# Scaling the normed rows of layer 1 on ACT instead of DVE

## The chip, the cores and the metric

The kernel runs on one core of one Trainium2 chip. The metric is device time in microseconds (us), the median of several runs. A core has five engines that run side by side, each with its own queue in program order: PE (TensorE, matrix products and transposes), DVE (VectorE), ACT (ScalarE), POOL (GpSimd) and SP, which here issues the DMAs.

## The reference

The input x has 8 images of 256 channels and 32 x 32 positions, all in float32. Layer 0 is a convolution and attention block on images. Layer 1 sees each image as 1024 tokens of 256 values and adds two branches to them, each behind a layer norm without weights:

```python
def _ln_t(v, eps=1e-5):
    m = jnp.mean(v, axis=-1, keepdims=True)
    s = jnp.var(v, axis=-1, keepdims=True)
    return (v - m) / jnp.sqrt(s + eps)

t = _to_tokens(x)
t = t + _L1_attn_ref(_ln_t(t), L1_attn_WQ, L1_attn_WK, L1_attn_WV)
t = t + _L1_ffn_ref(_ln_t(t), ...)
x = _from_tokens(t, x)
```

`_L1_attn_ref` is causal attention with one head over the 1024 tokens of an image. `_L1_ffn_ref` is a mixture of 8 experts of three products each, gated per token by a softmax over the mean of the normed tokens of all images. The change touches only the norm, `(v - m) / sqrt(s + eps)`.

## The kernel before

The kernel is written with a tile framework that places semaphores; every engine keeps the order in which the program issues its instructions. `pe`, `dve`, `act` and `pool` are thin wrappers that fix that order, and since all of them pass through one helper, almost all instructions have the line L73 in the profile. They are told apart by the tiles that they write and read.

Images are kept with the channels on the 128 partitions, in two halves (`KC` = 2), and the tokens along the free dimension. `layer_norm(src, dst, zt, room, bank)` norms the 1024 tokens of an image (8 rows of 128 tokens; two late calls take 4 rows) in these steps. PE transposes two rows at a time into a PSUM tile `tpt`, ACT copies it to `zt` (`zt_e` in the profile, one buffer for all calls; `scratch` in the last call), where a token is a partition. DVE takes mean and variance of each row (`st`, then `mv`). POOL makes the factor `r` = (variance + eps)^-0.5 for all rows at once, with one power and a step of refinement, six instructions on 8 columns, using the tile `y` on the way. Then `scaled(i0)` makes two rows `(row - mean) * factor` in place. PE transposes them back into `tpz`, and ACT copies `tpz` to `dst` (`z_e`, `z` or `z_last`).

`layer_norm` is a generator. Its steps are issued between those of a main stream by `together`, which weighs both by the microseconds that they yield. In layer 1's attention the main stream is `causal(b)`: eight score rows i of 128 queries for image b. For each, PE makes the scores `s`, DVE takes their negated maximum `nm`, ACT the exponential `pr`, DVE masks it (`lower`), sums it and inverts the sum (`rs`), POOL scales `pr` by `rs`, PE transposes it (`tp`), ACT copies that to `pT`, and every second row PE makes the product `po`, which DVE adds to the image (`te` or `t`). `tp` and half of the `tpt` and `tpz` tiles share one pair of PSUM buffers; `po`, `pk`, `pv` and the other half of `tpt` and `tpz` share another.

Beside image b's scores run, in this order, the first norm of image b + 1 (`first_norm`), the second norm of image b - 1 (`second_norm`), and the keys and values of image b + 1 (PE `pk`, `pv`, ACT copies `kk`, `v`); between them chores that split the experts' weights (`parts_w`). After a second norm POOL adds the normed image to `feat` in two halves, and ACT and DVE split it in two parts for the experts (`parts` on ACT, a subtraction to `parts` on DVE, then `z`):

```python
yield from layer_norm(t[b], z2, early["zt"], room, bank)
nc.sync.dma_start(u_d[b], t[b])
...
for h, feat in enumerate(feats):
    half = z2[:, :, h * HALF : (h + 1) * HALF]
    if b == 0:
        pool.tensor_copy(feat, half)
    else:
        pool.tensor_add(feat, feat, half)
```

The first norm of image 0 runs earlier, beside the end of layer 0 (PE `ph`, `py`, `rbn`, DVE `xn` there). The last image takes its score rows in reverse, beside the second norm of image 6 and then a norm of its own upper half (`last_norm`); its lower half is normed beside the first experts (`last_half`). After 2128 us the experts alone remain.

Of the kernel before, what the change touches and what calls it, by code (L numbers as in the profile page):

```python
# [12 lines left out]
AF = mybir.ActivationFunctionType  # L13
ALU = mybir.AluOpType
# [91 lines left out]
def conv_attn_hybrid_kernel(  # L106
# [368 lines left out]
    pe, dve = InOrder(tc, nc.tensor, TensorCost()), InOrder(tc, nc.vector, vector_cost)  # L475
    act, pool = InOrder(tc, nc.scalar), InOrder(tc, nc.gpsimd)
# [4 lines left out]
    def layer_norm(src, dst, zt, room, bank):  # L481

        n = src.shape[2] // P
        mv = room([P, NT, 2], "mv", 2)
        for i0 in range(0, n, 2):
            tp = bank([P, 2, C], "tpt")
            for i in range(2):
                for k in range(KC):
                    c0 = (i0 + i) * P
                    pe.transpose(tp[:, i, k * P : (k + 1) * P], src[:, k, c0 : c0 + P], ident)  # L490
            act.copy(zt[:, i0 : i0 + 2, :], tp)
            yield 0.6
            for i in range(i0, i0 + 2):
                st = room([P, 6], "st", 4)
                dve.bn_stats(st, zt[:, i, :])
                dve.bn_aggr(mv[:, i, :], st)
            yield 0.6

        y = room([P, NT], "y1", 2)[:, :n]
        r = room([P, NT], "r1", 2)[:, :n]  # L500
        pool.tensor_scalar(y, mv[:, :n, 1], LN_EPS, None, ALU.add)
        pool.tensor_tensor(r, y, mhalf1[:, :n], ALU.pow)
        pool.tensor_mul(y, y, r)
        pool.tensor_mul(y, y, r)
        pool.tensor_scalar(y, y, -0.5, 1.5, ALU.mult, ALU.add)
        pool.tensor_mul(r, r, y)

        for _ in range(4):
            yield 1.0

        def scaled(i0):
            for i in range(i0, i0 + 2):
                dve.tensor_scalar(zt[:, i, :], zt[:, i, :], mv[:, i, 0:1], r[:, i : i + 1], ALU.subtract, ALU.mult)

        scaled(0)
        yield 1.0
        scaled(2)
        yield 1.0
        for i0 in range(0, n, 2):
            if i0 + 4 < n:  # L520
                scaled(i0 + 4)
            tp = bank([P, KC, 2, P], "tpz")
            for i in range(2):
                for k in range(KC):
                    pe.transpose(tp[:, k, i, :], zt[:, i0 + i, k * P : (k + 1) * P], ident)
            act.copy(dst[:, :, i0 * P : (i0 + 2) * P], tp.rearrange("p k i c -> p k (i c)"))
            yield 0.9
# [42 lines left out]
    def first_tokens(early, bank, bank_kv):  # L570
        return (
            layer_norm(t[0], early["z"], early["zt"], early["room"], bank),
            keys_values(early["z"], early["kk"], early["v"], early["at"], early["wv"], bank_kv),
        )
# [798 lines left out]
    def tokens(stack, early, early_stack):  # L1373
# [85 lines left out]
        with ExitStack() as l1:  # L1459
# [94 lines left out]
            def first_norm(b):  # L1554
                z[b] = ring(b, "z", [P, KC, N])
                yield from layer_norm(t[b], z[b], early["zt"], room, bank)
# [12 lines left out]
            def second_norm(b):  # L1569
                yield from until((b, N // QC - 1))  # L1570
                z2 = two.tile([P, KC, N], F32, tag="z2", name="z2", bufs=1)
                yield from layer_norm(t[b], z2, early["zt"], room, bank)
                nc.sync.dma_start(u_d[b], t[b])
                if b + 3 < B:
                    load_t(b + 3)
# [6 lines that stand above are left out]
                for h in range(2):  # L1582
                    yield from z_parts(b, h, z2[:, :, h * HALF : (h + 1) * HALF])
# [473 lines left out]
```

## Time and profile before

| | us |
|---|---|
| median of 3 runs | 3111.16 |
| lowest, highest | 3108.97, 3123.86 |
| the profiled execution, and its span | 3114.98, 3113.2 |
| PE, DVE busy in the span | 2935.5 (94%), 2394.0 (77%) |
| ACT, POOL busy in the span | 1562.5 (50%), 311.1 (10%) |
| layer 1's attention, PE busy from 1470 to 1545 us | 71.77 of 75.00 |

The span is from the first to the last instruction of one execution. A group in the profile is a line, an engine, an operation, its tiles as out<-in, shapes and a count, then the busy time and the mean of one in ns, and behind a second bar the engine's idle time before them and who ended it. The chain is the sequence of waits that ended last, followed back from the end; a row in it has a start, a duration and the engine with its tile. A timeline row has a start, a duration, the engine, the instruction and a count of equal ones in a row, with the idle time before it in brackets. TensorE's granted clock is a share of its full speed.

### The profile page before, as it was taken

To read this page: it belongs to the slowest core of one execution; us is meant where nothing else is said; L and a number is where in the kernel's file an instruction comes from. 1 tells how busy PE (TensorE), PEld (TensorE's weight loads), DVE (VectorE), ACT (ScalarE), POOL (GpSimd) and SP (SyncE) were. 2 spreads that over 40 slices of the span, in tenths; PEclk is the share of its full clock that TensorE was granted. 3 is DMA by queue.
4 is the path that set the end of the run, shared out by engine and by line. 5 is a ranking of instruction groups with operands and counts; after the bars stand their busy time and mean duration, and the time that the engine had idled before them with its cause. 6 is when DMAs were issued, how large, how long until landed. Compare 5 with 4: busy or idle time off the path is not lost.

```text
span 3113.2 us, 41565 instructions
## 1 busy us (share of the span) xinstructions
PE 2935.5 (94%) x16802; PEld 1944.3 (62%) x16802; DVE 2394.0 (77%) x3014; ACT 1562.5 (50%) x2312; POOL 311.1 (10%) x419
## 2 busy tenths in 40 slices
PE   6988999999899989889999999899999999999998
PEld 4544555555555555456666666677777777777776
DVE  2378787878787879776676765698988888888887
ACT  3554454545454545333333333465666666666664
POOL 1012111111111110001122222000000000000000
PEclk8999999999999999989999999999999999999999
DMA  6202121211212120003332311411221152112210
GB/s 193 54 2 69 41 66 44 58 52 53 57 47 63 40 57 21 30 29 113 134 133 108 122 65 60 183 68 68 95 75 68 68 188 89 68 68 88 81 68 29
DMA packets 63856, 234.87 MB, mean 75 GB/s; under 512 B 5590, under 2 KB 13862, under 8 KB 54822
## 3 DMA queue, kind: packets, MB, share of 16 engines
q1 hardware_dynamic: 63654, 232.12, 22.8%
q8 instruction: 134, 2.20, 0.3%
q14 instruction: 68, 0.56, 0.1%
HBM read 140.61 MB, written 91.49 MB: 75 GB/s over the span
## 4 chain that ended last, share of the span: by engine, by line
PE 81%; DVE 13%; ACT 3%; DMA 1%; issue 1%; POOL 1%; SPq 0%; ACTq 0%; DVEq 0%
PE pm L73 12%; PE pa L73 11%; PE q L73 11%; PE po L73 11%; PE s L73 8%; PE ph L73 6%; DVE o L73 4%; PE pq L73 3%; PE sums L73 3%; PE pz L73 2%; DVE x L73 2%; PE pv L73 2%; PE pk L73 2%; PE pp L73 2%; DVE conv L73 1%; DVE zt_e L73 1%
## 5 line engine op out<-in xcount | busy, mean ns | idle before, releaser
L73 PE MATMUL pa<-ze,w 128*128 128x512 f32 x1488 | 423.1, 393 | 0.0
L73 DVE SCALAR_TENSOR_TENSOR x<-hpad,vec,x 128x1024 f32<-128x1024 f32 x248 | 316.7, 1283 | 73.2 <-ACT x L73 65.8
L73 DVE SCALAR_TENSOR_TENSOR conv<-hpad,vec,conv 128x1024 f32<-128x1024 f32 x256 | 327.4, 1282 | 19.0 <-ACT conv L73 12.9
L73 PEld LDWEIGHTS pa<-ze,w 128*128 128x128 f32 x1488 | 278.2, 188 | 63.3 <-issue 3.0
L73 ACT ACTIVATE h<-pa,bn_o,s1a 128x512 f32<-128x512 f32 x256 | 198.6, 776 | 203.4 <-PE pa L73 203.4
L73 ACT ACTIVATE pT<-s 128x1024 f32<-128x1024 f32 x256 | 247.9, 1024 | 93.7 <-PE s L73 93.5
L73 PE MATMUL po<-pT,vT 128*32 128x256 f32 x4096 | 271.0, 382 | 0.0
L73 PE MATMUL q<-h2p,w 128*128 128x512 f32 x768 | 269.0, 459 | 0.0
L73 DVE SCALAR_TENSOR_TENSOR h<-pa,s1b,h 128x512 f32<-128x512 f32 x256 | 191.2, 747 | 93.6 <-PE pa L73 85.5
L73 PE MATMUL ph<-xn,piw 128*128 128x512 f32 x512 | 239.9, 610 | 8.3 <-ACT x L73 4.0
L73 PE MATMUL pm<-h,w 128*128 128x512 f32 x512 | 240.8, 592 | 0.0
L73 PE MATMUL q<-z_first,w 128*128 128x512 f32 x768 | 217.1, 391 | 2.8 <-DVE z_first L73 1.7
L73 PE MATMUL pm<-h1p,w 128*128 128x512 f32 x768 | 216.7, 390 | 0.5 <-DVE h1p L73 0.5
L73 PEld LDWEIGHTS q<-h2p,w 128*128 128x128 f32 x768 | 144.6, 188 | 83.1 <-issue 59.3
L73 DVE SCALAR_TENSOR_TENSOR o<-vpad,pe_w,o 128x1024 f32<-128x1024 f32 x128 | 163.6, 1282 | 39.4 <-ACT o L73 36.3
L73 PE MATMUL s<-qst,kst 128*128 128x256 f32 x1024 | 177.1, 317 | 7.2 <-ACT pT L73 4.5
L73 PEld LDWEIGHTS po<-pT,vT 128*32 128x32 f32 x4096 | 120.0, 109 | 84.0 <-issue 2.4
L73 PEld LDWEIGHTS s<-qst,kst 128*128 128x128 f32 x1024 | 140.8, 199 | 44.9 <-issue 30.4
L73 PEld LDWEIGHTS ph<-xn,piw 128*128 128x128 f32 x512 | 92.7, 193 | 121.7 <-issue 97.8
L73 PEld LDWEIGHTS q<-z_first,w 128*128 128x128 f32 x768 | 144.4, 188 | 34.3 <-DVE z_first L73 2.9
L73 PEld LDWEIGHTS pm<-h1p,w 128*128 128x128 f32 x768 | 144.7, 188 | 31.7 <-DVE h1p L73 0.9
L73 PE MATMUL sums<-pT,ones 128*32 128x256 f32 x2048 | 157.4, 379 | 0.0
(280 smaller groups left out, 5121.1 us busy)
## 6 DMA issues: line engine op xcount, KB each, us to landing
ze<-zd SPq DMA_DIRECT2D x29, 1536.0 KB, 6.4
qst<-part SPq DMA_DIRECT2D x32, 512.0 KB, 9.5
kst<-part SPq DMA_DIRECT2D x32, 512.0 KB, 16.0
te<-ud SPq DMA_DIRECT2D x32, 512.0 KB, 4.1
wd<-parts_w SPq DMA_DIRECT2D x20, 768.0 KB, 3.7
w<-wd SPq DMA_DIRECT2D x20, 768.0 KB, 5.5
zd<-parts SPq DMA_DIRECT2D x14, 1024.0 KB, 3.8
ud<-te SPq DMA_DIRECT2D x18, 512.0 KB, 3.3
```

Source lines behind the costliest of these rows:

```text
L73: return self._tc.keep_in_program_order(method(*args, **kwargs))
```

## The change

After the factor POOL makes a term, minus mean times factor, for all rows with two further instructions on 8 columns, in the tile `y` that it used before. The two rows of `scaled` are then made by ACT, as row times factor plus term with factor and term as column operands, and no longer by DVE. It applies to every call of `layer_norm`, 128 rows in all.

```diff
@@ -504,13 +504,15 @@
         pool.tensor_mul(y, y, r)
         pool.tensor_scalar(y, y, -0.5, 1.5, ALU.mult, ALU.add)
         pool.tensor_mul(r, r, y)
+        pool.tensor_mul(y, mv[:, :n, 0], r)
+        pool.tensor_scalar(y, y, -1.0, 0.0, ALU.mult, ALU.add)
 
         for _ in range(4):
             yield 1.0
 
         def scaled(i0):
             for i in range(i0, i0 + 2):
-                dve.tensor_scalar(zt[:, i, :], zt[:, i, :], mv[:, i, 0:1], r[:, i : i + 1], ALU.subtract, ALU.mult)
+                act.activation(zt[:, i, :], zt[:, i, :], AF.Identity, bias=y[:, i : i + 1], scale=r[:, i : i + 1])
 
         scaled(0)
         yield 1.0
```

## The prediction

> **What bounds the kernel now.** I read the page's totals and chain first, then the groups of the row scaling and of what could do it on ACT, then the chain and the timeline of one image's stretch in layer 1. The page:
>
> ```profile
> PE 2935.5 (94%) x16802; PEld 1944.3 (62%) x16802; DVE 2394.0 (77%) x3014; ACT 1562.5 (50%) x2312; POOL 311.1 (10%) x419
> PE 81%; DVE 13%; ACT 3%; DMA 1%; issue 1%; POOL 1%; SPq 0%; ACTq 0%; DVEq 0%
> L73 DVE TENSOR_SCALAR zt_e<-zt_e,mv,r 128x256 f32<-128x256 f32 x124 | 61.9, 558 | 10.8 <-POOL r L73 10.8
> L73 DVE TENSOR_SCALAR zt_e<-zt_e,mv,r x124: 394/402/2423, 1280.4 to 1964.8; 128x256 f32<-128x256 f32 x124
> ```
>
> PE bounds the whole; DVE is 13% of the chain. The scaled rows (124 in zt_e and 4 in scratch) take 402 ns in the median, but 558 in the mean and 2423 at worst: something holds some of them. Layer 1's attention runs from 1395 to 1967 us, an image about every 75 us. In each stretch two norms run beside the scores: the first norm of the next image and the second norm of the previous one. The chain of waits, and the timeline (start, duration, engine, instruction), where a second norm ends:
>
> ```profile
> 1562.76 1.77 DVE zt_e L73 x4
> 1564.52 1.15 DVE nm L73
> ...
> 1568.37 3.58 DVE zt_e L73 x3
> 1571.95 0.14 issue
> 1572.08 1.09 PE tpz L73 x4
> 1573.17 3.96 PE po L73 x16
> ```
> ```profile
> 1568.28 3.98 DVE L73 TENSOR_SCALAR zt_e<-zt_e,mv,r 128x256 f32<-128x256 f32 x4
> 1568.54 0.91 POOL L73 TENSOR_SCALAR pr<-pr,rs 128x768 f32<-128x768 f32 x1 [4.80 <-DVE rs L73]
> 1569.42 2.37 POOL L73 TENSOR_TENSOR feat<-feat,z 128x1024 f32<-128x1024 f32 x1
> 1572.08 1.09 PE L73 MATMUL tpz<-ident,zt_e 128*128 128x128 f32 x4 [1.99 <-DVE zt_e L73]
> 1573.87 2.36 POOL L73 TENSOR_TENSOR feat<-feat,z 128x1024 f32<-128x1024 f32 x1 [2.08 <-ACT z L73]
> 1575.68 1.63 DVE L73 TENSOR_TENSOR parts<-z,parts 128x1024 f32<-128x1024 f32 x1 [2.29 <-ACT parts L73]
> ```
>
> From 1553 to 1572 us DVE is the chain, with 1.8 + 3.6 us of scaled rows in it, and PE stands still for most of 1567 to 1572. The rows that last 1.0 and 2.4 us coincide with POOL's pr and feat. This recurs near 1643, 1718, 1793 and 1869 us (second norms of images 1 to 5); for image 0 the chain shows 2.27 us there, its feat being a short copy. The first norms are the other kind; between the scores the chain is PE alone:
>
> ```profile
> 1533.37 2.08 DVE L73 TENSOR_SCALAR zt_e<-zt_e,mv,r 128x256 f32<-128x256 f32 x6 [1.07 <-POOL r L73]
> 1534.69 0.60 PE L73 MATMUL tpz<-ident,zt_e 128*128 128x128 f32 x4
> 1537.72 1.05 PE L73 MATMUL tpz<-ident,zt_e 128*128 128x128 f32 x8
> ```
>
> Here DVE's rows are just in time and cost nothing.
>
> **The change part by part.** *Removed:* 128 rows from DVE, 0.33 us from one to the next when unheld. *Added on ACT:* 128 activations of 256 columns with two column operands. The trace has none; nearest is conv<-ph with both operands at 512 columns, 771 ns; less 256 columns at 0.83 ns (h<-h 625 at 512, x<-x 1050 at 1024) gives 558; from o<-vpad, 1236 at 1024, 599. I take 585. ACT's pairs overlap by about 0.1 (two copies of 0.59 in 1.07), so 0.49 from row to row: eight rows are 4.0 us of ACT. The total, some 70 us, lies beside other work in a half-idle engine; only its place in the queue matters. *Added on POOL:* two operations on 8 columns before the rows may start; the like ones last 0.20 and start 0.28 apart: 0.56 us later. No DMA is added or moved. No table load: Identity on yr and hi alternates with Exp in layer 0, and the kernel has 17 loads in all.
>
> The Trainium skill speaks against this ("ScalarE: Activation LUTs", Rules for kernel authors: multiply and add belong on VectorE). By it, each norm loses 8 x (0.49 - 0.33) + 0.56 = 1.8 us wherever its rows are on the path; 16 norms, 29 us slower, about 3140. The trace says otherwise for the second norms: there the eight DVE rows cost 5.4 us of chain. So I replay each kind on the trace's times.
>
> *Second norms, images 1 to 5.* POOL's factor is ready at 1562.42, its term at 1563.0. ACT, idle since 1561.55, does four rows by 1565.1 and then the pr that was at 1565.75, from 1565.0: 0.7 earlier. The two DVE-row groups vanish; pr, one pT copy, rows 4 and 5, a z copy and rows 6 and 7 follow on ACT until 1568.8, so PE turns the last rows at 1568.9 in place of 1572.1 and starts po 3.6 earlier. The granted clock, 0.75 from 1570 to 1573 and 0.68 to 1576 after PE's pause, need not fall either: po then lasts 3.1 and not 4.0. PE alone would gain 4.5. But look at what is late next. ACT's parts ends at 1572.2, and DVE's parts subtraction then meets the second feat of POOL, which now starts at 1571.8, straight after the first. The 1.63 above is 0.54 of waiting for feat and 1.09 of work; at 1941.0 the same subtraction took 2.88 beside feat. The Trainium skill ("SBUF — State Buffer", SBUF: two separate sides) has an exclusive lock between GpSimd and a DVE operation with two SBUF inputs, held for a whole instruction, ACT having its own ports: so rows on ACT are never held, but the subtraction is held to 1574.1. Without the lock the sum is 4.5 per image, with it this: subtraction done 1575.2, te, lower, the masked row and z done 1578.6, so nm of the last score row starts at 1578.6, before at 1581.14. Behind it on ACT are pr and the kk copy for which PE's third pk group waits (PEld waited 0.50 for it at 1584.87). Gain 2.5 each: 12.5.
>
> *Second norm of image 0:* the feat copies (1.09, 1.04) are over before the subtraction; gain 2.7.
>
> *First norms, images 2 to 7.* POOL's term comes at 1533.9, rows 0 and 1 end at 1535.05, PE wanted them at 1534.69: 0.4 lost. Rows 2 to 5 hold up z, pr and two pT copies; the first pT copy ends at 1538.35, not 1537.63, and frees the PSUM tile that PE wants at 1538.1: 0.25 more. Nothing later in the stretch gives it back, since PE is the chain until 1552. 6 x 0.65 = 3.9 lost. Bounds: 0, if the order of the tiles spares the second wait and POOL is quicker, and 4.5, all of ACT's 4.0 and POOL's 0.56. *Image 1's* (1410 us) is DVE's chain with rows lengthened by pr (0.68, 0.79 for 0.40): tpz at 1415.99 becomes free of waits, 0.9 gained.
>
> *Second norm of image 6* (the last stretch, scores in reverse) is already a POOL-to-rows-to-copies chain:
>
> ```profile
> 1935.03 2.67 DVE L73 TENSOR_SCALAR zt_e<-zt_e,mv,r 128x256 f32<-128x256 f32 x8 [2.16 <-POOL r L73]
> 1936.91 1.56 ACT L73 COPY z<-tpz 128x512 f32<-128x512 f32 x3 [3.26 <-PE tpz L73]
> 1939.40 3.44 PE s L73 x8
> ```
>
> Rows and copies now share ACT: rows 0 to 5 from 1935.6 to 1938.6, the third z copy to 1941.1 in place of 1938.5, so the scores start 2.6 later; with PE idle that long I add 0.9 for a half-clock stretch: 3.5 lost.
>
> *The rest:* image 0's first norm at 1281 us: 0.3 lost (POOL's delay; DVE's xn comes earlier). The two half norms: about 0.4 lost together, covered mostly by PE; without cover they cost 2 x (2.0 + 0.56) = 5.
>
> Sum: 12.5 + 2.7 + 0.9 - 3.9 - 3.5 - 0.7 = 8.0 us faster. The profiled execution took 3114.98 (span 3113.2); less 8.0 it is 3107. The median of the runs, 3111.16, lies 3.8 lower; from it: 3103.
>
> **The rivals.** *No lock in the way:* the subtraction gets in before the second feat, or ACT's rows are quicker, and PE's 4.5 comes through: 5 x 4.5 + 3.2 + 0.9 - 3.9 - 3.5 - 0.7 = 18.5, time 3093. For it: at image 6 the subtraction asked during the first feat (1941.0) and its end, 1943.9, less 1.09 of work, says that it was let in at 1942.8, between the two. Against: parts is four ACT operations (2.8 us) behind the z copy that starts feat (2.4 us), so it comes 0.4 us too late.
>
> *ACT's queue becomes the bound of the first norms* (the slower side): six rows stand in front of z, pr and the pT copies, and PE waits for these in order. At the full price of 4.5 each, 11.9 - 6 x 4.5 = 15 slower (11.9 is the sum without first norms' loss), time 3126; were the second norms' gain lost too (pr behind the rows there as well), 3141. It decides from 2.0 us a norm on, where 11.9 is used up. For it: the waits of PE there are zero now and ACT serves PE's tiles. Against: ACT had 3.2 us free before z there, and PE has 16 transposes and 8 score matmuls in between.
>
> *It doesn't reach the path at all:* DVE's order after 1572 is kept by other waits (te after po), so second norms gain what first norms lose; 3111.
>
> **How the numbers follow.** This kernel's measurement can tell about 0.5%, 15.6 us: faster is below 3095.6, slower above 3126.7. My forecast (3097 to 3109) has 0.45, the path unmoved (3108 to 3116) 0.15, no lock 0.24, ACT's queue 0.16. Of the forecast's chance 0.04 lies below 3095.6, of the queue's 0.12 above 3126.7, of the unmoved 0.01. The range reaches into both sides: 3089 to 3124.
>
> **What would show it.** In the changed profile: a row on ACT near 585 ns; no DVE TENSOR_SCALAR on zt_e; PE's wait before the last tpz of a second norm under 1 us where it was 1.99; parts on DVE 2.5 to 3.0 us instead of 1.63; the half-clock stretches of images 1 to 5 gone; PE waiting about 2 us in pk for ACT's kk copy; in first norms a PE wait of 0.4 for ACT zt_e; stretches near 73.2 us in place of 75.1. I am wrong if these stretches keep 75 us, or if first norms show PE waits over 2 us.

## The result and the profile after

The changed kernel takes 3104.35 us in the median of 21 runs (3098.13 to 3113.97), the kernel before 3114.41 in 21 runs beside it (3107.97 to 3127.12). The ratio is 0.9966, with a 95% interval of 0.9956 to 0.9975: 8 to 14 us faster, the middle near 10.6. The profiled executions are 12.1 us apart in span (3113.2 and 3101.1). The page after, and the new rows among the groups of tile zt_e (duration in ns: least, median, most):

```profile
PE 2927.2 (94%) x16802; PEld 1930.9 (62%) x16802; DVE 2339.8 (75%) x2886; ACT 1620.6 (52%) x2440; POOL 316.8 (10%) x453
PE 74%; DVE 14%; ACT 6%; POOL 2%; DMA 2%; issue 1%; SPq 0%; ACTq 0%; DVEq 0%; POOLq 0%
L73 ACT ACTIVATE zt_e<-zt_e,y,r x124: 583/588/614, 1280.0 to 1954.6; 128x256 f32<-128x256 f32 x124
```

A row on ACT is slower than the unheld row on DVE (588 against 402 ns), but none is long: the worst is 614, where DVE's worst was 2423. DVE has 54 us less to do and ACT 58 more, yet PE still bounds the kernel. The page cannot say where 10 us went; the timeline of the second norm of image 1 can (the place shown before at 1568 to 1577):

```profile
1561.22 2.08 ACT L73 ACTIVATE zt_e<-zt_e,y,r 128x256 f32<-128x256 f32 x4 [1.47 <-POOL y L73]
1566.57 0.93 PE L73 MATMUL tpz<-ident,zt_e 128*128 128x128 f32 x4 [0.53 <-ACT zt_e L73]
1567.55 4.68 POOL L73 TENSOR_TENSOR feat<-feat,z 128x1024 f32<-128x1024 f32 x2 [0.62 <-ACT z L73]
1570.32 3.00 DVE L73 TENSOR_TENSOR parts<-z,parts 128x1024 f32<-128x1024 f32 x1 [3.33 <-ACT parts L73]
1575.01 3.60 PE L73 MATMUL pk<-z,at 128*128 128x512 f32 x8
1576.73 1.22 DVE L73 TENSOR_REDUCE nm<-s 128x1 f32<-128x1024 f32 x1
1580.44 3.70 PE L73 MATMUL pk<-z,at 128*128 128x512 f32 x8 [1.83 <-ACT kk L73]
```

PE's wait for the last rows fell from 1.99 us to 0.53. But POOL's two additions to feat now run back to back, DVE's subtraction, which asks during the second of them, grew from 1.63 to 3.00 us, and PE, which used to run through pk, stands 1.83 us in it. The chain of waits in this stretch shows how the two are joined:

```profile
1570.32 3.00 DVE parts L73
...
1575.58 1.23 DVE z L73
1576.81 1.15 DVE nm L73
...
1578.04 1.11 ACT pr L73
1579.15 0.75 ACT pT L73 x2
1579.90 0.50 ACT kk L73
1580.40 0.04 issue
1580.44 3.70 PE pk L73 x8
```

The subtraction holds up nm of the last score row, nm the exponential, and the kk copy stands behind that in ACT's queue. So a good part of the gain became a new wait. The first norms, which had no wait on PE, now have a small one (timeline of the first norm of image 3, the place shown before at 1533 to 1538):

```profile
1531.47 3.06 ACT L73 ACTIVATE zt_e<-zt_e,y,r 128x256 f32<-128x256 f32 x6 [1.82 <-POOL y L73]
1532.24 0.81 PE L73 MATMUL tpz<-ident,zt_e 128*128 128x128 f32 x4
1535.89 1.09 PE L73 MATMUL tpz<-ident,zt_e 128*128 128x128 f32 x8 [0.24 <-ACT pT L73]
```

To add this up I take, from the profiled executions, the time from the first pk of one image to that of the next, with the start of layer 1's scores ahead and the first lg (the gate) behind. "Chosen", "later" and "both" are experiments told below.

| from, to | before | after | chosen | later | both |
|---|---|---|---|---|---|
| scores, image 1 | 28.60 | 27.57 | 27.54 | 27.57 | 27.32 |
| image 1, 2 | 84.82 | 82.36 | 81.71 | 82.37 | 81.69 |
| image 2, 3 | 74.83 | 70.96 | 70.34 | 71.00 | 70.30 |
| image 3, 4 | 74.96 | 72.79 | 72.13 | 71.11 | 70.35 |
| image 4, 5 | 75.03 | 72.74 | 72.11 | 71.00 | 70.32 |
| image 5, 6 | 75.06 | 72.79 | 72.16 | 71.04 | 70.36 |
| image 6, 7 | 75.38 | 74.58 | 73.07 | 72.84 | 71.28 |
| image 7, gate | 85.68 | 89.84 | 87.48 | 89.79 | 86.21 |
| sum | 574.36 | 563.63 | 556.53 | 556.72 | 547.83 |

Of the 12.1 us between the spans, 10.7 lie here. The stall in pk comes after an image's first pk, so it counts to the next line: image 2 to 3 shows the gain without it (3.9 with the first norm's loss), image 7 to the gate a stall that belongs to image 5's norm.

### The profile page after: what moved, and what is told of

Its sections match the earlier page's. It is cut to its first block, busy times and chain, and to the rows that moved or that the text cites. A ratio compares the mean times of both kernels' runs of the same rounds, so it can differ in the third digit from the quotient of the medians.

```text
span 3101.1 us, 41593 instructions
## 1 busy us (share of the span) xinstructions
PE 2927.2 (94%) x16802; PEld 1930.9 (62%) x16802; DVE 2339.8 (75%) x2886; ACT 1620.6 (52%) x2440; POOL 316.8 (10%) x453
## 4 chain that ended last, share of the span: by engine, by line
PE 74%; DVE 14%; ACT 6%; POOL 2%; DMA 2%; issue 1%; SPq 0%; ACTq 0%; DVEq 0%; POOLq 0%
PE pm L73 12%; PE pa L73 11%; PE q L73 11%; PE po L73 9%; PE s L73 6%; PE ph L73 6%; DVE o L73 4%; PE pq L73 3%; PE sums L73 3%; DVE conv L73 3%; DVE x L73 2%; PE pz L73 2%; ACT zt_e L73 2%; PE pv L73 2%; PE pp L73 1%
```

## The experiments

**Which norms gain.** In four kernels a call of `layer_norm` says whether ACT or DVE makes its rows; POOL makes the term only for ACT. What they share, shown with the choice of the first:

```diff
-    def layer_norm(src, dst, zt, room, bank):
+    def layer_norm(src, dst, zt, room, bank, on_act=False):
...
+        if on_act:
+            pool.tensor_mul(y, mv[:, :n, 0], r)
+            pool.tensor_scalar(y, y, -1.0, 0.0, ALU.mult, ALU.add)
...
+                if on_act:
+                    act.activation(zt[:, i, :], zt[:, i, :], AF.Identity, bias=y[:, i : i + 1], scale=r[:, i : i + 1])
+                else:
+                    dve.tensor_scalar(zt[:, i, :], zt[:, i, :], mv[:, i, 0:1], r[:, i : i + 1], ALU.subtract, ALU.mult)
...
-                yield from layer_norm(t[b], z[b], early["zt"], room, bank)
+                yield from layer_norm(t[b], z[b], early["zt"], room, bank, False)
...
-                yield from layer_norm(t[b], z2, early["zt"], room, bank)
+                yield from layer_norm(t[b], z2, early["zt"], room, bank, b < 6)
```

*Second norms of images 0 to 5.* 

> ACT scales the rows only in the second norms of images 0 to 5, DVE everywhere else. Theory (the terms of the prediction are separate and add up): 5 x 2.5 + 2.7 = 15.2 us faster than before, ratio near 0.9951, and faster than the full change by 5 to 7 us; stretch from one image's first pk to the next about 72.2 us. Rival A (the gain comes from DVE being relieved as a whole, wherever its rows lie): about half of the full change's gain, 5 us, ratio 0.9984. Rival B (the second norms gain nothing by themselves; the stretches are shorter for another reason, such as image 1's norm or the clock): within 2 us of before.

Measured: 0.9948 (0.9933 to 0.9963), 16 us faster, where the theory has 15.2. The stretches from image 2 to 5 last 70.3, 72.1 and 72.1 us, as under "chosen" in the table, but the next, from image 5 to 6, lasts 74.9 and not 72.2. There one order was turned round (timeline):

```profile
1712.79 1.01 POOL L73 TENSOR_SCALAR pr<-pr,rs 128x896 f32<-128x896 f32 x1 [3.58 <-DVE rs L73]
1712.91 1.96 DVE L73 SCALAR_TENSOR_TENSOR z<-parts 128x1024 f32<-128x1024 f32 x1 [0.29 <-issue]
1718.50 5.40 PE L73 MATMUL pk<-z,at 128*128 128x512 f32 x8 [2.92 <-ACT kk L73]
```

At the same place in every other norm of images 1 to 5, in every kernel here, DVE's z starts first and takes 1.2 us, and POOL's pr, which starts during it, takes 1.8 to 1.9. Here z came 0.3 us late and POOL was first: pr took 1.01 and z 1.96, PE waited 2.92 in pk and not 1.84, and ran the rest of pk at half clock (5.40 us for 3.70). The stretches add up to 560.24 us, 14.1 less than before, or 16.9 without this. The relief of DVE as a whole is ruled out as the cause: its 0.9984 lies outside the interval, and with 48 of the 128 rows moved the stretches are 3.4 us shorter than with all.

*First norms of images 2 to 7 only* (`b >= 2` in the first call, `False` in the second). 

> ACT scales the rows only in the first norms of images 2 to 7, DVE everywhere else. Theory: PE waits 0.4 us for the first ACT rows and 0.25 us for a PSUM tile that the later pT copy frees, 0.65 a norm, so 3.9 us slower than before, ratio 1.0013; the half-clock stretches of the second norms are there as before. Rival A (relief of DVE as a whole): about 5 us faster, ratio 0.9984. Rival C (ACT's queue becomes the bound of first norms): 2 us or more a norm, over 12 us slower, ratio 1.004 or more.

Measured: 1.001 (0.9999 to 1.002), 3 us slower in the middle, where the theory has 3.9; ACT's queue as the bound (1.004) and a gain (0.9984) both lie outside the interval. The timeline of the first norm of image 3 and a line of the waits (us in total, times, longest) show the price on PE:

```profile
1540.76 0.82 PE L73 MATMUL tpz<-ident,zt_e 128*128 128x128 f32 x4
1544.42 1.09 PE L73 MATMUL tpz<-ident,zt_e 128*128 128x128 f32 x8 [0.25 <-ACT pT L73]
```
```profile
PEld tpz L73 <- ACT zt_e L73: 4.8, 12, 0.6
```

From the first of these groups to the second it is now 3.66 us and was 3.03 (1534.69 to 1537.72 before): 0.63 a norm. Of it 0.22 is in the first group, which lasts 0.82 instead of 0.60 while its weight loads wait for ACT's rows, and 0.41 comes ahead of the second, where the profile shows a wait of 0.25 for the pT copy that frees its tile (the other 0.16 is the overlap with the scores before it). One expectation failed: the half-clock stretches of the second norms were not there as before, but in this execution (3128.84 us, where the median of the kernel's 13 runs is 3122.16) three of the five of images 1 to 5 last 6.8 us where before's last 3.4. So its stretches add up to 582.92 us, 8.6 more than before, of which 0.63 a norm makes 3.8; whether the longer half-clock stretches come of the change is open.

*Second norm of image 6 only* (`False` and `b == 6`). 

> ACT scales the rows only in the second norm of image 6, DVE everywhere else. Theory: rows and z copies share ACT there, the last image's scores start later by 2.6 us and 0.9 us for a slower clock: 3.5 us slower than before, ratio 1.0011; the trace of the full change loses about 4 us in that stretch, its last norm included, so 3 to 4. Rival A (relief of DVE as a whole): nothing or a gain of 0.6 us. If the loss seen after the full change belongs to the last norm and not to image 6, this run equals before.

Measured: 0.9993 (0.9984 to 1.0003). The whole time does not show the loss, but the trace does. ACT's part of the timeline:

```profile
1935.17 3.06 ACT L73 ACTIVATE zt_e<-zt_e,y,r 128x256 f32<-128x256 f32 x6 [1.94 <-POOL y L73]
1938.14 0.56 ACT L73 COPY z<-tpz 128x512 f32<-128x512 f32 x1
1938.61 1.09 ACT L73 ACTIVATE zt_e<-zt_e,y,r 128x256 f32<-128x256 f32 x2
1939.60 1.04 ACT L73 COPY z<-tpz 128x512 f32<-128x512 f32 x2
```

Rows and copies take turns on ACT, and from the first pk of image 7 to the gate it is 88.28 us instead of 85.68: 2.60 lost, as the theory said without its 0.9 for the clock. After the gate the two programs are equal, yet this execution is 2.4 us quicker there than before's (1143.03 to 1145.46 us), with fewer stretches at half clock. I put that down to chance of the clock: over the 65 runs of these four kernels and of before beside them a straight line of time on mean granted clock, with an offset for each kernel, gives 1.6 us less for each 0.001 of clock, and this kernel's runs had 0.9735 in the mean where before's had 0.9706. At an equal clock the line puts it 2.1 us (plus or minus 1.2) slower than before. (The same line puts the kernel with first norms alone 5.4 slower, plus or minus 1.1, and the chosen norms 14.9 faster, plus or minus 1.7. It is no better measure than the ratio there: a kernel that adds or removes half-clock stretches moves its own clock, and the line takes that part out.) So the place and size of the loss are shown by the trace; the ratio by itself decides nothing.

*Chosen: second norms of images 0 to 5 and the first norm of image 1* (`b == 1` and `b < 6`). 

> ACT scales the rows in the second norms of images 0 to 5 and in the first norm of image 1, DVE in all others. Theory: 12.5 + 2.7 + 0.9 = 16.1 us faster than before, ratio 0.9948, 8 us (by the trace of the full change 6 to 8) faster than the full change. If the terms don't add (rival A), it lies between before and the full change, at 0.997 or above.

Measured: 0.9937 (0.9924 to 0.995), 20 us faster than before; the expected 0.9948 lies inside the interval, at its slow end, and by the table the sum is 17.8 faster (574.36 to 556.53). The terms add up, and the choice beats the full change by 7.1 us in the table.

**Whether POOL's feat is what holds DVE.** Two kernels leave the additions of images 1 to 7 to feat out, so the experts' gate sees image 0 alone; one has the rows on DVE, one on ACT.

```diff
                     if b == 0:
                         pool.tensor_copy(feat, half)
-                    else:
-                        pool.tensor_add(feat, feat, half)
```

*Rows on DVE, without feat.* 

> The kernel before (DVE scales the rows) without POOL's additions of the normed images 1 to 7 to feat, so the sum over images is left out. Theory (POOL's feat holds DVE's rows while it runs): the last three rows of a second norm take 1.2 us and not 3.6, and no row of these norms lasts 2.4 us; PE starts po about 2.4 us earlier, so 2.4 to 3 us for each of images 1 to 5, 12 to 15 us faster than before, ratio 0.995 to 0.996, nearly what the full change brings. Rival D (feat and the rows only coincide; the rows are long for another reason): the long rows stay, within 2 us of before.

Measured: 0.9953 (0.9939 to 0.9967), 14.6 us faster. The groups of zt_e on DVE, and the timeline of the same second norm:

```profile
L73 DVE TENSOR_SCALAR zt_e<-zt_e,mv,r x124: 394/403/1115, 1281.1 to 1949.2; 128x256 f32<-128x256 f32 x124
```
```profile
1567.52 1.95 DVE L73 TENSOR_SCALAR zt_e<-zt_e,mv,r 128x256 f32<-128x256 f32 x4
1567.97 0.44 PE L73 MATMUL tpz<-ident,zt_e 128*128 128x128 f32 x2 [1.67 <-DVE zt_e L73]
1572.69 1.23 DVE L73 TENSOR_TENSOR parts<-z,parts 128x1024 f32<-128x1024 f32 x1 [2.08 <-ACT parts L73]
```

The four rows that took 3.98 us take 1.95, and the worst row of all is 1115 ns instead of 2423. That one lies beside POOL's copy to feat for image 0, which stays; beside pr rows still take up to 1004. In before's trace 72 of the 124 rows have no POOL instruction beside them, and none of these takes more than 414 ns, while every row above 900 has one. That the rows and feat only coincide is ruled out. In these norms DVE did not have too much to do; it was held.

*Rows on ACT, without feat.* 

> The full change (ACT scales the rows) without POOL's additions of the normed images 1 to 7 to feat, so the sum over images is left out. Theory (the second feat holds DVE's subtraction for parts): the subtraction takes 1.1 us and not 3.0, the wait of PE in pk for ACT's kk copy shrinks from 1.8 us to nearly 0, and what the prediction called PE's 4.5 us per image comes through in place of 2.5: 10 us faster than the full change, 18 to 20 us faster than before, ratio 0.994. Rival D (no hold): same as the full change, ratio 0.9966.

Measured: 0.9947 (0.9934 to 0.996), 16.5 us faster than before. The expected 0.994 lies inside the interval, though near its fast end. All 14 subtractions are now short, and PE runs through pk (timeline, ten matmuls in a row):

```profile
L73 DVE TENSOR_TENSOR parts<-z,parts x14: 1205/1221/1226, 1501.2 to 1933.8; 128x1024 f32<-128x1024 f32 x14
```
```profile
1579.45 4.76 PE L73 MATMUL pk<-z,at 128*128 128x512 f32 x10
```

Its stretches of images 3 to 6 last 71.1 us, 1.65 less than after, where the expectation had 2.0. All its stretches add up to 557.01 us, 17.4 less than before. What else is missing of the expected 18 to 20 us lies from image 7 to the gate: 89.87 us, no less than after's 89.84 although the stall is gone, with a half-clock stretch of 3.4 us from 1922.4 that after does not have.

**Moving the hold away.** All work is kept; the second addition is issued behind the first half's parts.

```diff
                     else:
                         pool.tensor_add(feat, feat, half)
-                for h in range(2):
-                    yield from z_parts(b, h, z2[:, :, h * HALF : (h + 1) * HALF])
+                    yield from z_parts(b, h, half)
```

*Later: this on the full change.* 

> The full change with POOL's second feat addition issued after the first half's parts work instead of straight after the first addition; all work is kept. Theory: the first subtraction on DVE no longer meets feat, it takes 1.1 to 1.6 us, nm of the last score row comes up to 1.9 us earlier, PE's wait in pk for kk shrinks: up to 2 us per image, 5 to 10 us faster than the full change, ratio to before 0.9935 to 0.995. Rival E (the hold only moves, to the second subtraction, to te or to the mask, and ends as late): same as the full change, 0.9966.

Measured: 0.9938 (0.9925 to 0.9952), 19 us faster than before, so about 9 faster than the full change. The timeline of the same place:

```profile
1569.54 2.36 POOL L73 TENSOR_TENSOR feat<-feat,z 128x1024 f32<-128x1024 f32 x1 [0.62 <-ACT z L73]
1572.31 1.23 DVE L73 TENSOR_TENSOR parts<-z,parts 128x1024 f32<-128x1024 f32 x1 [3.34 <-ACT parts L73]
1576.99 7.37 PE L73 MATMUL pk<-z,at 128*128 128x512 f32 x16
1577.88 2.35 POOL L73 TENSOR_TENSOR feat<-feat,z 128x1024 f32<-128x1024 f32 x1
1579.40 0.97 DVE L73 TENSOR_TENSOR pr<-pr,lower 128x128 f32<-128x128 f32 x1 [1.24 <-ACT pr L73]
```

The subtraction takes 1.23 us, pk runs through, and the stretches are as short as without any feat (71.0 to 71.1). Rival E was half right: the hold did move, to the mask of the last score row (0.97 us; it takes 0.29 where feat is left out), but PE has pk in front of it there and does not wait. In image 6's norm, where the two halves follow faster, it moved to the second subtraction (2.80 us for 1.22).

*Both: the chosen norms and feat later.* 

> ACT rows only in the second norms of images 0 to 5 and the first norm of image 1, and the second feat addition issued after the first half's parts work. Theory: the gain of the chosen norms (0.9937 of before measured) and up to 2 us more per image: 25 to 29 us faster than before, ratio 0.991 to 0.992. Rival E (the hold only moves): 0.9937.

Measured: 0.9913 (0.9898 to 0.9928), 27 us faster than before and faster than every other kernel here: 3090.21 us in the median where before took 3114.7 beside it, and its slowest run (3092.12) lies below the fastest of "later" (3093.87). In image 6's norm, with the rows on DVE, both subtractions are held (2.87 and 2.80 us). Its page:

```profile
PE 2936.1 (95%) x16802; PEld 1944.2 (63%) x16802; DVE 2360.3 (76%) x2958; ACT 1587.3 (51%) x2368; POOL 313.6 (10%) x433
PE 78%; DVE 13%; ACT 4%; DMA 2%; issue 1%; POOL 1%; SPq 0%; ACTq 0%; DVEq 0%; POOLq 0%
```

ACT's share of the chain is 4%, after the full change it was 6%. The busy time of the engines in one window of 75 us says the same, first of before, then of after, then of this kernel (us, then PE, PEld, DVE, ACT, POOL, granted clock, DMA share, GB/s):

```profile
1590.00:1665.00 75.00, 70.22 (x294) 46.62 (x293) 53.98 (x121) 25.92 (x46) 17.77 (x22) 0.98 0.34 127
```
```profile
1590.00:1665.00 75.00, 71.73 (x301) 46.77 (x300) 47.82 (x106) 33.77 (x63) 18.50 (x26) 1.00 0.35 129
```
```profile
1590.00:1665.00 75.00, 73.73 (x312) 48.77 (x311) 49.19 (x114) 30.89 (x57) 18.08 (x24) 1.00 0.38 141
```

PE's idle time in 75 us goes from 4.8 to 3.3 to 1.3.

## Why the prediction was right

The change gained what was forecast, a little more (8.0 us predicted, 10.1 between the medians), and by the forecast mechanism: four terms of five are within about a fifth, one is off by a third. That 3103 and 3104.35 lie so close is in part luck. The 3103 starts from 3111.16, the median of three runs, where before has 3114.41 over 21, and this 3.3 and the gain that was 2.1 too small nearly cancel; from 3114.41 the forecast would have been 3106.4. In the column "shown", a term is a difference of the table's columns.

| term of the sum, us gained | predicted | shown | by |
|---|---|---|---|
| second norms, images 1 to 5 | 12.5 | 13.7 | before less chosen, image 2 to the gate |
| second norm, image 0 | 2.7 | 3.1 | before less chosen, image 1 to 2 |
| first norm, image 1 | 0.9 | 1.0 | before less after, scores to image 1 |
| first norms, images 2 to 7 | -3.9 | -4.7 | chosen less after, image 1 to 7 |
| second norm, image 6 | -3.5 | -2.4 | chosen less after, image 7 to the gate |
| sum of these | 8.7 | 10.7 | before less after |

The terms shown are taken along one chain of kernels, so they must add up to 10.7. That they are separate is tested by the kernels that move one kind alone: the second norms of images 0 to 5 give 14.1 (16.9 without the turned order) where the table has 13.7 + 3.1, and image 6's gives -2.6 where it has -2.4, a figure with the last image's half norm in it.

*Second norms.* Counted from the last score product that both have in common (1562.52 before, 1560.72 after), PE starts po 3.8 us earlier (predicted 3.6) and, since po no longer runs into a half-clock stretch (it takes 3.2 us and not 4.2), starts pk 4.8 earlier (predicted 4.5). The stall in pk gives back 1.83 (predicted about 2). That is 3.0 for this norm where the sum had 2.5; the five together gave 13.7 for 12.5. The prediction's decisive choice, the value with the lock in place of the one without, is what the trace and the experiments confirm most directly: the subtraction asked 0.45 us after the second feat had begun (1570.32 and 1569.87), where the prediction had 0.4; with feat gone or moved the rest of the 4.5 comes through, and the 18.5 us of "no lock in the way" are what moving feat brought (17.8 between the medians), not what the change did.

*The hold.* The prediction took from the Trainium skill ("SBUF — State Buffer", SBUF: two separate sides) that GpSimd and a DVE operation of this kind exclude one another for a whole instruction. Both sides of it are now measured: the subtraction takes 1.23 us alone and 3.00 when it asks during feat, and it asked at 1570.32 where feat ended at 1572.23, so it waited 1.9 and worked 1.1; and POOL's pr takes 1.01 alone and 1.8 to 1.9 when it asks during DVE's z. The prediction took the rule for operations with two inputs in SBUF; the rows, with one such input and two column operands, were held as well. ACT's rows were never longer than 614 ns, though some run beside POOL's pr (in the kernel with feat later, two rows from 1567.89 to 1568.99 and pr from 1568.02 to 1568.92). From the rule that spoke against the change (the Trainium skill, "ScalarE: Activation LUTs", Rules for kernel authors: add and multiply belong on VectorE) the prediction had worked out 29 us slower; its premise, that a row on DVE is the faster one, is true of the median (402 against 588 ns) and false where POOL is at work.

*First norms.* The loss of 0.65 was met in five of six norms (0.62 to 0.66), but by two errors that cancel: the rows cost 0.22 and not 0.4, and the second group comes 0.41 later and not 0.25. For image 7 it was 1.51, the term's mis-sized part: there another transpose meets a z copy that stands behind the rows (timeline of after, then of the chosen norms, where the rows of this norm are on DVE):

```profile
1826.34 0.66 PE L73 MATMUL tp<-ident,pr 128*128 128x128 f32 x4 [1.56 <-ACT z L73]
```
```profile
1820.55 0.65 PE L73 MATMUL tp<-ident,pr 128*128 128x128 f32 x4 [0.24 <-ACT z L73]
```

The wait grew from 0.24 to 1.56 us. "ACT's queue becomes the bound" thus had its mechanism, at 0.8 us a norm on average and far from its 2.0.

*Image 6.* Of the 3.5, the 2.6 for shared ACT was right (2.4 and 2.6). The 0.9 for a half-clock stretch did not come in this execution nor in that of the image 6 experiment; in those of the two kernels without feat on ACT and with feat later such a stretch of 3.4 us is there, from 1922.4 and 1922.3. In two of four executions, then. Where it came it cost about 1.8 by the table (89.87 without feat, where after's 89.84 less its stall of 1.8 would be 88.0), so that 0.9 is near the mean of the four, though it was written as the cost of one stretch. The term missed because this execution drew none.

*The rest.* The -0.7 for image 0 and the half norms can't be told from the clock. The start of layer 1's scores is 0.8 later than before, but it varies from 1387 to 1399 us between before and the first three experiments, which are the same up to there. After the gate the changed kernel is 2.1 quicker, but kernels with equal instructions there differ by 3.3 (1142.15 to 1145.46).

*What would show it.* The signs came: the row at 588 ns, no TENSOR_SCALAR on zt_e, a wait of 0.53 before the last tpz, parts at 3.00, no half-clock stretch in these five stretches, a pk wait of 1.83, stretches of 72.8 us. Only the wait for zt_e in first norms is on PE's weight loads and not on its matmuls.

## What to carry to other kernels

Before moving work off a busy engine, ask whether it is busy or held: a group whose longest instruction is six times its median, always beside another engine's instruction, may be held, as here, where moving or removing either party helped. Follow what the released engine starts earlier, here feat meeting the subtraction: the new collision took two fifths of what PE gained in a second norm, and moving one issue undid it. And decide call by call, since one helper serves places where DVE is late and places where ACT is; here the six chosen second norms and one first norm were worth more than all sixteen.

## What the runs showed of the hardware

POOL holds DVE, and the held instruction is shown as a long one and not as a wait. A 128x128 mask on DVE takes 0.29 us alone and 0.97 when it starts in the last 0.8 us of feat. Even a DVE operation with a single large operand (a row with two column operands) is held: up to 414 ns alone, 1006 beside pr, 1117 beside the copy to feat and 2423 beside the addition to feat. Which of the two waits is decided by who starts first: POOL's pr of 896 columns took 1.01 us and DVE's z 1.96 where POOL was first, and 1.8 to 1.9 and 1.2 where DVE was. A start 0.3 us later turned this round once and cost 2.8 us.

In layer 1's attention half-clock stretches last 3.4, 6.8, 10.2 or 13.7 us, and where they fall differs between executions of equal instructions. One result is that a loss of 2.6 us in one place, plain in the trace, can vanish from a ratio with an interval of plus or minus 3 us; the other is that pauses removed from PE paid twice here, by themselves and by the clock: po took 4.17 us before and 3.20 after.
